# Layer 0's dependencies regrouped, and an expert's first 256 tokens multiplied with the down weights in seven block products instead of eight

## The chip, the cores and the metric

The kernel runs on one core of a Trainium2 chip. Its engines work at the same time, each through its own list of instructions in order: TensorE (PE) multiplies matrices, VectorE (DVE) and ScalarE (ACT) do elementwise work and read the results out of PSUM, GpSimd (POOL) issues gathers and scatters, and SyncE (SP) issues the plain transfers. They wait for each other by semaphores. The metric is the device time of one execution in microseconds (us), the median of several.

## The reference

The input is a matrix x of 625 nodes by 1024, and 10,625 edges (src, dst), among them a loop for every node. Two layers follow, each added to its input.

```
h    = layernorm(x)
h1   = relu(h @ W_self0 + mean(h) @ W_neigh0 + b0)
x    = x + h1 @ W_self1 + mean(h1) @ W_neigh1 + b1
f    = layernorm(x)
w    = softmax(f @ gate.T), kept for the two largest of 8 experts
out  = sum over experts e of w[:, e] * ((silu(f @ G[e].T) * (f @ U[e].T)) @ Dn[e].T)
x    = x + out + sigmoid(f @ s) * shared(f)
```

`mean` is the mean over a node's incoming edges. An expert has 1408 inner columns: G[e] and U[e] are 1408 x 1024, Dn[e] is 1024 x 1408. Everything is in f32.

## The kernel before

**Nodes and layer 0.** The 625 nodes lie in five tiles of 125. While PE multiplies the normalised rows with W_neigh0 (`rows_times`, tile y0), DVE writes one-hot rows of the edges, and PE counts edges between nodes with them, packed in digits. If a count does not fit its digit, the count is made anew in another way. So there is a region "count" with two cases, chosen by a register: case 1 recounts (`count_anew`, tile at), case 0 does nothing of it. In both cases PE multiplies the last rows of y0 (`last_rows`, eight products on bank 5), so that the choice has work beside it, and in case 0 ACT casts the counts c16 to bf16 (tile cb). Then h @ W_self0 is computed transposed (h1T) in seven block products for eight (`block_product`, bank p_h); DVE makes the sums of blocks for it (w3, b3 and in place), and y0 is split into three bf16 parts zh, zm, zl (`split`, with the scratch tiles yr). Region "sum0" then multiplies the parts with the counts: two halves of the nodes by eight groups of 128 columns, 15 matmuls a group; DVE scales each group by the reciprocal degree, adds it to h1T and takes the maximum with 0. Layer 1 follows in the same manner, from h1T, with the region "sum1".

**Experts.** One region for each of eight experts. Its case is the number of 64-token units that the expert has tokens for, from 0 (up to 64 tokens) to 7 (up to 512); `full` is the number of whole units of 128, and `odd` says that a half unit of 64 is left over. An expert's gathered rows are transposed into xg; the gate and up products fill ht (inner columns in 11 chunks of 128, tokens along the free dimension). The down stage multiplies ht with the weights wd, 11 chunks of 128 x 1024 that were loaded in full: first the half unit (`down_unit`), then the units from the last to the first (`down`, j = 3 to 0). A unit has two halves of 512 output columns, each 11 products into one bank; banks are 6 and 7, swapped if there is a half unit. ACT drains the first half, DVE the second, both with the routing weight as scale, into ys[j % 2] (the half unit uses ys[2]), and POOL scatters the unit's rows, adding to the output in memory. `CUT` parts the second half of unit 0: the weights' first six chunks are free once it has passed them, and SP then issues their loads for the next expert; the other five follow behind the region. The transposes of the next expert's first unit are put ahead of the down stage, on banks 2 and 3; those of its second unit come at the next region's start, on banks 4 and 5.

**Order and dependencies.** Python functions record all operations in one order (`Rec.op`); each engine gets its own in that order, and waits are derived from the tiles' bytes. In PSUM they go by bank: an operation waits for the last operation of every other engine on the bank, whether it reads or writes.

```
deps.update(o for e, o in m.bank[b].items() if e != eng or writing and eng != "PE")
```

A region's cases are recorded one beside the other and emitted as a branch. Since the case is not known before, an operation outside the case that depends on one inside waits for the end of its *segment* on that engine. `Rec.point` closes a segment: its end on an engine is the last instruction so far that the engine has in the region, and the counts of all cases are made equal there.

```
self.ends[self.segment, e] = self.add(eng=e, kind="end", members=[last[e] for last in self.last])
```

Ahead of each branch, `hint` names the case that will be taken. `mm` records each matmul by itself (the profile's line 539), `mm_all` (547) and `some_chunks` (1489) a whole group. In the profile 503, 504, 507 and 511 are DVE helpers, 515 and 520 ACT's, 1287 and 1356 gather and scatter.

Of the kernel before, what the change touches and what calls it, by code (L numbers as in the profile page):

```python
# [15 lines left out]
N = 625  # L16
# [15 lines left out]
NE = 8  # L32
FF = 1408
FC = FF // 128
SI = 176
SC = 2
SP = SI // SC
# [264 lines left out]
def gnn_moe(nc, x, src, dst, w_gnn0, w_gnn1, b0, b1, w_gu, w_down, ws_up, ws_down, out):  # L302
# [18 lines left out]
    def slot(i):  # L321
        return i * SLOT
# [66 lines left out]
    yr = [p(f"yr{i}", [TP, BANK]) for i in range(2)]  # L389
    p = space(slot(2), slot(8))  # L390
# [54 lines left out]
    power = power_i.bitcast(FP)  # L445

    wg = sb("wg", [128, FC, KD, 2, 128], FP, slot(0))
    wd = [sb(f"wd{c}", [128, D], FP, slot(2 * FC + c)) for c in range(FC)]
    p = space(R2, R4 + 20480)
    xg = p("xg", [128, KD, CAP])  # L450
    ht = p("ht", [128, FC, CAP])
# [3 lines left out]
    p = space(R1, R2)  # L455
    ys = [p(f"ys{i}", [128, D]) for i in range(3)]
    rows = [*(rows012[:, j, :] for j in range(3)), p("rows3", [128, XW])][:NTL]

    pa = pb("pa", 0, (128, NT, DIG))
    pg = pb("pg", 0, (128, NT, BANK))  # L460
# [39 lines left out]
    def ts(o, i, s1, s2, op0, op1=None):  # L500
        aps = [i] + [s for s in (s1, s2) if isinstance(s, bass.AP)]
        if op1 is None:
            return k.op("DVE", lambda h: h.tensor_scalar(o, i, s1, None, op0=op0), r=aps, w=[o])  # L503
        return k.op("DVE", lambda h: h.tensor_scalar(o, i, s1, s2, op0=op0, op1=op1), r=aps, w=[o])
# [4 lines left out]
    def stt(o, a, s, b, op0, op1):  # L509
        aps = [a, b] + ([s] if isinstance(s, bass.AP) else [])  # L510
        return k.op("DVE", lambda h: h.scalar_tensor_tensor(o, a, s, b, op0=op0, op1=op1), r=aps, w=[o])

    def copy(o, i, eng="DVE"):
        if eng == "ACT":
            return k.op("ACT", lambda h: h.copy(o, i), r=[i], w=[o])  # L515
        return k.op("DVE", lambda h: h.tensor_copy(o, i), r=[i], w=[o])  # L516
# [18 lines left out]
    def mm(o, pairs, start=True, stop=True):  # L535

        for n, (a, b) in enumerate(pairs):
            s, e = start and n == 0, stop and n == len(pairs) - 1
            k.op("PE", lambda h, a=a, b=b, s=s, e=e: h.matmul(o, a, b, start=s, stop=e, skip_group_check=True),  # L539
                 r=[a, b], w=[o])  # L540
# [302 lines left out]
    def node_half(m, n):  # L843
        return h1T[:, m, n * HB:min(N, n * HB + HB)]
# [39 lines left out]


    k.open("sum0", 2)
    turn = 0
    for k.cls in range(2):
        for n, (n0, nn) in enumerate(HALVES):
            for c in range(KD):  # L890
                q, o, t = bank("p_sum", 4 + turn % 4)[:, :nn], node_half(c, n), summed[turn % 2][:, :nn]
                turn += 1
# [12 lines left out]
    for c in range(KD):  # L905
        load(ws1[:, c, :], w_gnn1[c])
# [572 lines left out]

    FIRST, LAST = 2, 4  # L1480

    CUT = 6

    def some_chunks(o, pairs, lo, hi):

# [32 lines left out]
    def down(e, j, between, swap, stages):  # L1518
        y, w = ys[j % 2], gw[:, e % 2, j:j + 1]
        q = [bank("p_down", 7 - half if swap else 6 + half) for half in range(2)]  # L1520
        pairs = [[(ht[:, c, j * 128:(j + 1) * 128], wd[c][:, lo:lo + BANK]) for c in range(FC)] for lo in (0, BANK)]
        if 0 in stages:
            in_parts(q[:1], pairs[:1], between)
            act(y[:, :BANK], q[0], AF.Copy, scale=w)
            some_chunks(q[1:], pairs[1:], 0, CUT)
        if 1 in stages:
            some_chunks(q[1:], pairs[1:], CUT, FC)
            ts(y[:, BANK:], q[1], w, None, ALU.mult)

    SEG = -(-FC // 4)  # L1530
    for e in range(NE):
# [68 lines left out]
        if more:  # L1600
# [50 lines left out]
    def more(i):  # L1651
        return nc.If(nc.values_load(cnt_i[0:1, i:i + 1], min_val=0, max_val=N) > CAP)
# [65 lines left out]
```

## Time and profile before

| | us |
|---|---|
| median of 3 runs (lowest, highest) | 1123.2 (1121.39, 1125.63) |
| the profiled execution | 1122.52 |
| its span, first to last instruction | 1120.7 |
| PE busy in it | 1080.1 |
| DVE, ACT, POOL busy | 289.4, 127.5, 50.2 |
| layer 0, to the end of sum0's matmuls | about 202 |
| down stage of the expert with width 432 | 677.94 to 744.28 |
| down stages of the two experts with width 224 | 908.04 to 945.81, 1014.65 to 1052.42 |

The mean granted PE clock is 0.990. The timeline shows the eight experts' cases by their instructions: in order, 2, 0, 6, 1, 0, 3, 3 and 1. So three have two whole units or more: the third expert (width 432, three whole units and a half one) and the sixth and seventh (width 224, two whole units). In the profile a matmul on f32 is two records, with a weight load each. A line of the timeline gives the start, the duration, the engine, the line of the code, the operation and its tiles, and in brackets how long the engine had been idle and what ended that. "issue" means that the engine waited for nothing the profile can name.

### The profile page before, as it was taken

How to read it: one execution, taken by the hardware profiler on the slowest of the kernel's cores; microseconds unless marked ns; L12 is line 12 of the kernel's file. 1: busy time of each engine (PE TensorE's matmuls, PEld its weight loads, DVE VectorE, ACT ScalarE, POOL GpSimd, SP SyncE). 2: the span in 40 equal slices, each digit the busy share in tenths (PEclk: the TensorE clock that was granted, in tenths of full speed). 3: DMA queues.
4: the chain of work that ended last, by engine and by line, in shares of the span. 5: the costliest groups of instructions: out<-in, count | busy, mean ns of one | idle time of the engine just before them, and what ended most of it. 6: DMA issues, size and time to landing. Idle time of an engine off the chain costs nothing.

```text
span 1120.7 us, 10853 instructions
## 1 busy us (share of the span) xinstructions
PE 1080.1 (96%) x4265; PEld 617.0 (55%) x4265; DVE 289.4 (26%) x718; ACT 127.5 (11%) x246; POOL 50.2 (4%) x56
## 2 busy tenths in 40 slices
PE   6998999999999989999899999999989999999996
PEld 3554776444555544544455554445449965995452
DVE  7963555664644450001000000001010000000000
ACT  1122320122000231011100000001010000000010
POOL 0000000000000040001000000100100001000001
PEclk9999999999999989999899999999999999999998
DMA  9600012302033239869953033168799644642601
GB/s 302 244 1 5 0 40 73 151 0 80 1 133 128 74 124 331 323 266 347 405 202 150 7 144 123 19 212 354 264 407 364 252 177 150 230 187 114 214 34 26
DMA packets 40874, 186.53 MB, mean 166 GB/s; under 512 B 6933, under 2 KB 6933, under 8 KB 29300
## 3 DMA queue, kind: packets, MB, share of 16 engines
q1 hardware_dynamic: 34432, 168.18, 38.9%
q0 software_dynamic: 6000, 16.26, 6.3%
q8 instruction: 62, 1.02, 0.4%
q14 instruction: 120, 0.98, 0.3%
q10 hardware_dynamic: 260, 0.09, 0.0%
HBM read 170.51 MB, written 13.99 MB: 165 GB/s over the span
## 4 chain that ended last, share of the span: by engine, by line
PE 92%; DVE 3%; issue 3%; ACT 1%; DMA 1%; POOL 0%; SPq 0%; POOLq 0%; ACTq 0%; DVEq 0%
PE p_gu L547 34%; PE p_down L1489 20%; PE p_y L539 11%; PE p_h L539 5%; PE p_sage L539 5%; PE p_gu L1422 5%; PE p_sum L539 5%; PE p_gs L539 2%; PE p_downs L539 1%; PE pa L656 1%; PE p_gu L597 1%; PE p_tr L597 1%; DVE ln_st L554 1%; DMA rows<-xfw,idx 0%; DMA xa<-in_x_dram 0%
## 5 line engine op out<-in xcount | busy, mean ns | idle before, releaser
L547 PE MATMUL p_gu<-xg,wg 128*128 128x224 f32 (+1 forms) x1056 | 264.2, 413 | 0.4 <-ACT xg L515 0.2
L547 PEld LDWEIGHTS p_gu<-xg,wg 128*128 128x128 f32 x1056 | 201.3, 191 | 62.8 <-issue 61.4
L1489 PE MATMUL p_down<-wd,ht 128*128 128x512 f32 (+1 forms) x616 | 229.5, 594 | 0.0
L1489 PEld LDWEIGHTS p_down<-wd,ht 128*128 128x128 f32 (+1 forms) x616 | 95.0, 175 | 125.0 <-issue 124.8
L507 DVE TENSOR_TENSOR ht<-ht,p_gu 128x256 f32<-128x256 f32 (+3 forms) x63 | 27.4, 437 | 368.9 <-PE p_gu L547 231.8
L547 PE MATMUL p_gu<-wg,xg 128*128 128x512 f32 (+1 forms) x288 | 116.8, 565 | 0.9 <-DVE ht L507 0.6
L547 PEld LDWEIGHTS p_gu<-wg,xg 128*128 128x128 f32 x288 | 55.1, 193 | 60.1 <-issue 57.7
L539 PE MATMUL p_y<-wn,h0T 128*125 128x512 f32 x160 | 72.8, 610 | 1.3 <-ACT h0T L515 1.3
L520 ACT ACTIVATE ht<-p_gu 128x256 f32<-128x256 f32 (+3 forms) x63 | 25.0, 396 | 428.7 <-PE p_gu L547 357.8
L1422 PE MATMUL p_gu<-wg,xg 128*64 128x512 f32 (+2 forms) x384 | 58.3, 461 | 0.5 <-ACT xg L515 0.5
L503 DVE TENSOR_SCALAR ys<-p_down,gw 128x512 f32<-128x512 f32 x10 | 7.5, 751 | 182.6 <-PE p_down L1489 182.6
L539 PE MATMUL p_h<-h0T,ws 128*128 128x313 f32 x192 | 51.1, 426 | 3.4 <-issue 3.4
L539 PEld LDWEIGHTS p_y<-wn,h0T 128*125 128x125 f32 x160 | 30.1, 193 | 37.9 <-issue 35.2
L539 PEld LDWEIGHTS p_h<-h0T,ws 128*128 128x128 f32 x192 | 36.2, 189 | 18.4 <-issue 4.2
L1356 POOL DMA_INDIRECT out_dram<-ys,idx x13 | 19.9, 1532 | 556.6 <-DVE ys L503 320.8
L1422 PEld LDWEIGHTS p_gu<-wg,xg 128*64 128x64 f32 x384 | 25.5, 137 | 32.1 <-issue 28.1
L539 PE MATMUL p_y<-wn,h1T 128*125 128x512 f32 x96 | 41.6, 593 | 1.5 <-DVE h1T L503 1.5
L539 PE MATMUL p_sage<-ws,h1T 128*125 128x512 f32 x96 | 41.9, 592 | 0.0
L503 DVE TENSOR_SCALAR os<-node,src_f 125x640 f16<-125x640 f16 x85 | 32.2, 379 | 3.0 <-PE pa L656 3.0
L539 PEld LDWEIGHTS p_y<-wn,h1T 128*125 128x125 f32 x96 | 17.9, 188 | 24.5 <-issue 22.2
L539 PEld LDWEIGHTS p_sage<-ws,h1T 128*125 128x125 f32 x96 | 17.9, 187 | 22.1 <-issue 21.8
L539 PE MATMUL p_gs<-wus,xfT 128*125 128x361 f32 x80 | 25.2, 467 | 0.4 <-DVE xfT L516 0.4
(202 smaller groups left out, 778.2 us busy)
## 6 DMA issues: line engine op xcount, KB each, us to landing
wg<-in_w_gu_dram SPq DMA_DIRECT2D x88, 1024.0 KB, 10.8
wd<-in_w_down_dram SPq DMA_DIRECT2D x88, 512.0 KB, 9.5
wn<-in_w_gnn_dram SPq DMA_DIRECT2D x16, 512.0 KB, 13.8
ws<-in_w_gnn_dram SPq DMA_DIRECT2D x16, 512.0 KB, 13.5
xr<-in_x_dram SPq DMA_DIRECT2D x5, 448.0 KB
xfw<-xf SPq DMA_DIRECT2D x5, 448.0 KB
out_dram<-xr SPq DMA_DIRECT2D x5, 448.0 KB
xa<-in_x_dram SPq DMA_DIRECT2D x4, 448.0 KB
```

Of the source, the lines that this page charges most:

```text
L503: return k.op("DVE", lambda h: h.tensor_scalar(o, i, s1, None, op0=op0), r=aps, w=[o])
L507: return k.op("DVE", lambda h: h.tensor_tensor(o, a, b, op), r=[a, b], w=[o])
L520: return k.op("ACT", lambda h: h.activation(o, i, f, **kw), r=aps, w=[o])
L539: k.op("PE", lambda h, a=a, b=b, s=s, e=e: h.matmul(o, a, b, start=s, stop=e, skip_group_check=True), r=[a, b], w=[o])
L547: got = h.matmul(o if m is None else o[:, :m], a, b if m is None else b[:, :m], start=start and n == 0, stop=stop and n == len(pairs) - 1, ...
L554: k.op("DVE", lambda h, part=part, st=st: h.bn_stats(st, part), r=[part], w=[st])
L597: got = h.transpose(pt[:, c, :], i[:n, (4 * g + c) * 128:(4 * g + c + 1) * 128], ident[:n, :n])
L656: k.op("PE", lambda h, s=s: h.matmul(pa[:, s, :], o_s[:, s, :], o_d[:, :DIG], start=c == 0 and s == 0, stop=c == EC - 1 and s == NT - 1, s ...
L1356: h.indirect_dma_start(out=to, out_offset=bass.IndirectOffsetOnAxis(ap=i, axis=0), in_=y, in_offset=None, compute_op=ALU.add).then_inc(s, 16)
L1422: got = h.matmul(o, *pairs[n], start=n == 0, stop=n == len(pairs) - 1, skip_group_check=True)
L1489: got = h.matmul(o[job], *pairs[job][n], start=n == 0, stop=n == FC - 1, skip_group_check=True)
```

## The change

**Layer 0.** Four edits. `last_rows` is cut in two by inner chunks: the first four chunks stay in the count region's first segment, the other four come in a second segment that both cases share, with a one-element copy on DVE so that the engine has an end there. The cast to cb comes before the last rows' copy, and cb lies at R3 now, over the recount's tile at, instead of over the weights wn0. yr moves to slot 7, and deg_row, w3, b3 and the tiles `summed` from slot 2 to slot 0. Region sum0 is ordered by halves outside and cases inside, with a segment end behind each half, and its groups go round all eight banks instead of four.

**Down stage.** If an expert has two whole units or more, units 1 and 0 are multiplied together (`down_pair`). The 256 tokens by 10 chunks of ht and the 10 chunks by 1024 columns of wd are each cut in 2 x 2 blocks (128 tokens, 5 chunks, 512 columns), and seven products of sums of blocks replace eight products of blocks. DVE makes the sums, most of them in place in ht and wd, e3 in a new tile and the fifth block difference d3 in parts of xg that are free by then. The eleventh chunk is multiplied in the plain way, one product for each of the four blocks of the result. The first product's bank z (6) is drained three times into ys as a beginning, is added to by the second product and drained once more; the others (x, y, w: banks 4, 5, 7) are added to ys by DVE with the routing weight. Stage 0 uses the weights' first five chunks for the last time, so `CUT` becomes 5 for all. Units 3 and 2 and the half unit are as before. Unit 1's scatter is issued behind unit 0's end, next to unit 0's.

```
-    p = space(slot(0), slot(8))
-    cb = p("cb", [TP, NT, N], BF)
+    cb = sb("cb", [TP, NT, N], BF, R3)
+    p = space(slot(0), slot(8))
...
-    def last_rows():
+    def last_rows(part):
         q = bank("p_y", 5)[:TP, :]
-        mm(q, [(h0T[:, c, N - TP:N], wn0[:, c, BANK:]) for c in range(KD)])
-        copy(y0[:, NT - 1, BANK:], q, "ACT")
+        mm(q, [(h0T[:, c, N - TP:N], wn0[:, c, BANK:]) for c in range(KQ * part, KQ * part + KQ)], part == 0, part == 1)
+        if part:
+            copy(y0[:, NT - 1, BANK:], q, "ACT")
...
     count_anew()
-    last_rows()
+    last_rows(0)
     k.cls = 0
     copy(ok[:, 1:2], ok[:, 0:1])
-    last_rows()
     copy(cb, c16[:, :, :N], "ACT")
+    last_rows(0)
+    k.cls = None
+    k.point()
+    for k.cls in range(2):
+        last_rows(1)
+        copy(ok[:, 2:3], ok[:, 0:1])
...
-    for k.cls in range(2):
-        for n, (n0, nn) in enumerate(HALVES):
+    for n, (n0, nn) in enumerate(HALVES):
+        for k.cls in range(2):
             for c in range(KD):
-                q, o, t = bank("p_sum", 4 + turn % 4)[:, :nn], node_half(c, n), summed[turn % 2][:, :nn]
+                q, o, t = bank("p_sum", (4 + c) % 8)[:, :nn], node_half(c, n), summed[c % 2][:, :nn]
...
-    k.cls = None
-    k.point()
+        k.cls = None
+        k.point()
...
-    CUT = 6
+    CUT = FD
...
+    def down_pair(e, stages):
+        a11, a12, a21, a22 = (ht[:, i:i + FD, t:t + 128] for t in (0, 128) for i in (0, FD))
+        b11, b12, b21, b22 = (wd_all[:, i:i + FD, n:n + BANK] for i in (0, FD) for n in (0, BANK))
+        x, y, w, z = (bank("p_down", b) for b in (4, 5, 7, 6))
...
+        if 0 in stages:
+            tt(e3, a11, a21, ALU.subtract)
+            tt(a21, a21, a22, ALU.add)
+            for i, o in enumerate(d3):
...
+                    tt(o, hi, lo, ALU.subtract)
+            product(z, a11, b11, True)
+            act(place(0, 1), z, AF.Copy, scale=by[0])
+            ts(place(1, 0), z, by[1], None, ALU.mult)
+            act(place(1, 1), z, AF.Copy, scale=by[1])
+            tt(b12, b12, b11, ALU.subtract)
+            product(z, a12, b21, False, (0, 0))
+            act(place(0, 0), z, AF.Copy, scale=by[0])
+            tt(a11, a21, a11, ALU.subtract)
+            tt(b11, b22, b12, ALU.subtract)
+            tt(a12, a12, a11, ALU.subtract)
+            tt(b21, b21, b11, ALU.subtract)
+            product(y, a21, b12, True)
+            more(1, 1, y)
+            product(x, a11, b11, True)
+            more(0, 1, x)
+            product(w, None, None, True, (1, 1))
+            more(1, 1, w)
+        if 1 in stages:
+            product(x, e3, d3, False)
+            more(1, 1, x)
+            product(y, a12, b22, False, (0, 1))
+            more(0, 1, y)
+            product(x, a22, b21, False, (1, 0))
+            more(1, 0, x)
...
-        for j, stages in ((None, (0, 1)), *((j, (0, 1)) for j in range(NTL - 1, 0, -1)), (0, (0,)), (0, (1,))):
+        for j, stages in ((None, (0, 1)), *((j, (0, 1)) for j in range(NTL - 1, 1, -1)), (0, (0,)), (0, (1,))):
...
+                elif j == 0 and full > 1:
+                    down_pair(e, stages)
...
-                now.append(scatter(e, j, half))
+                now += [scatter(e, i, half) for i in ((0, 1) if j == 0 else (j,))]
```

Here `tt` is a sum or difference on DVE, `ts` and `act` scale a bank into a tile on DVE and ACT, `place(j, half)` is a half of ys[j], `more(j, half, q)` adds bank q, scaled, to it on DVE, and `product(q, a, b, start, last)` multiplies two blocks into a bank, with the eleventh chunk's product behind them if `last` is given.

More of the change, by code (lines that the diff above doesn't have):

```diff
@@ L34 @@
 FC = FF // 128
+FD = FC // 2
 SI = 176
@@ L385, in gnn_moe @@
     t3 = p("t3", [128, KQ, BANK])
+    cb = sb("cb", [TP, NT, N], BF, R3)
     p = space(slot(0), slot(8))
-    cb = p("cb", [TP, NT, N], BF)
     yh, ym = (p(n, [TP, NT, D], BF) for n in ("yh", "ym"))
-    yr = [p(f"yr{i}", [TP, BANK]) for i in range(2)]
-    p = space(slot(2), slot(8))
+    yr = [sb(f"yr{i}", [TP, BANK], FP, slot(7) + 2048 * i) for i in range(2)]
+    p = space(slot(0), slot(8))
     deg_row, w3, b3 = p("deg_row", [128, N]), p("w3", [128, KQ, BANK]), p("b3", [128, KQ, HB])
@@ L447, in gnn_moe @@
     wg = sb("wg", [128, FC, KD, 2, 128], FP, slot(0))
-    wd = [sb(f"wd{c}", [128, D], FP, slot(2 * FC + c)) for c in range(FC)]
+    wd_all = sb("wd", [128, FC, D], FP, slot(2 * FC))
+    wd = [wd_all[:, c, :] for c in range(FC)]
     p = space(R2, R4 + 20480)
@@ L457, in gnn_moe @@
     rows = [*(rows012[:, j, :] for j in range(3)), p("rows3", [128, XW])][:NTL]
+    e3 = p("e3", [128, FD, 128])
+    d3 = [xg[:, 2 * i:2 * i + 2, 128:384] for i in range(4)] + [xg[:, :4, 384:]]
     pa = pb("pa", 0, (128, NT, DIG))
@@ L886, in gnn_moe @@
     k.open("sum0", 2)
-    turn = 0
-    for k.cls in range(2):
-        for n, (n0, nn) in enumerate(HALVES):
+    for n, (n0, nn) in enumerate(HALVES):
+        for k.cls in range(2):
             for c in range(KD):
-                q, o, t = bank("p_sum", 4 + turn % 4)[:, :nn], node_half(c, n), summed[turn % 2][:, :nn]
-                turn += 1
+                q, o, t = bank("p_sum", (4 + c) % 8)[:, :nn], node_half(c, n), summed[c % 2][:, :nn]
                 cols = slice(c * 128, (c + 1) * 128)
@@ L1528, in down, with product, place, more @@
             ts(y[:, BANK:], q[1], w, None, ALU.mult)
+    def down_pair(e, stages):
+        a11, a12, a21, a22 = (ht[:, i:i + FD, t:t + 128] for t in (0, 128) for i in (0, FD))
+        b11, b12, b21, b22 = (wd_all[:, i:i + FD, n:n + BANK] for i in (0, FD) for n in (0, BANK))
+        x, y, w, z = (bank("p_down", b) for b in (4, 5, 7, 6))
+        by = [gw[:, e % 2, j:j + 1] for j in range(2)]
+        def product(q, a, b, start, last=None):
+            pairs = [(a[:, i, :], b[i] if isinstance(b, list) else b[:, i, :]) for i in range(FD)] if a is not None else []
+            if last is not None:
+                j, half = last
+                pairs.append((ht[:, FC - 1, 128 * j:128 * j + 128], wd[FC - 1][:, half * BANK:half * BANK + BANK]))
+            mm_all(q, pairs, start=start)
+        def place(j, half):
+            return ys[j][:, half * BANK:half * BANK + BANK]
+        def more(j, half, q):
+            o = place(j, half)
+            stt(o, q, by[j], o, ALU.mult, ALU.add)
+        if 0 in stages:
+            tt(e3, a11, a21, ALU.subtract)
+            tt(a21, a21, a22, ALU.add)
+            for i, o in enumerate(d3):
+                if i in (0, 4):
+                    m = 4 if i == 0 else 1
+                    o = xg[:, :, 128:384] if i == 0 else o
+                    o = o.rearrange("p (k a) b -> p k a b", k=m)
+                    hi, lo = (b[:, i:i + m, :].rearrange("p k (a b) -> p k a b", b=o.shape[-1]) for b in (b22, b12))
+                    tt(o, hi, lo, ALU.subtract)
[23 more added lines that the diff above has]
+            more(1, 0, x)
```

## The prediction, made before the result was known

> **What bounds the kernel now.** I read the page's busy times and its chain first: they say which engine sets the end, and whether anything else can be on the path.
>
> ```profile
> PE 1080.1 (96%) x4265; PEld 617.0 (55%) x4265; DVE 289.4 (26%) x718; ACT 127.5 (11%) x246; POOL 50.2 (4%) x56
> ...
> PE 92%; DVE 3%; issue 3%; ACT 1%; DMA 1%; POOL 0%; SPq 0%; POOLq 0%; ACTq 0%; DVEq 0%
> ```
>
> The matmul engine carries 92% of the chain. So the change can win in two ways: fewer matmuls, or less time in which PE stands still. The list of what PE waited for prices the second way.
>
> ```profile
> PE p_xg L597 <- issue: 7.5, 2, 4.0
> PE p_h L539 <- issue: 3.4, 1, 3.4
> ...
> PE p_y L539 <- DVE h1T L503: 1.5, 1, 1.5
> PE p_sum L539 <- DVE summed L507: 1.4, 1, 1.4
> ```
>
> Three of these lie in layer 0, which the change touches: 3.4, 1.5 and 1.4 us. The first says "issue", which names no releaser, so I looked at the other engines in time order around it.
>
> ```profile
> 105.74 0.58 ACT L515 COPY y<-p_y 125x512 f32<-125x512 f32 x1 [6.28 <-PE p_y L539]
> ...
> 106.22 2.80 ACT L515 CAST cb<-c 125x3125 bf16<-125x3125 f16 x1
> ...
> 109.12 17.09 PE L539 MATMUL p_h<-h0T,ws 128*128 128x313 f32 x64 [3.42 <-issue]
> ```
>
> The cast to cb ends at 109.02 and PE goes on at 109.12. In the code p_h takes banks that the recount (the other case of the region) drains on ACT, and after a region such a dependency is on the segment's last ACT instruction: the cast. PE waits for cb, which it needs only 60 us later.
>
> Last, the down stages of the experts with two full units or more. The timeline shows three: the expert at 547 us (width 432, three full units and a half one), and those at 840 and 947 us (width 224, two).
>
> ```profile
> 706.72 0.75 DVE L503 TENSOR_SCALAR ys<-p_down,gw 128x512 f32<-128x512 f32 x1 [17.56 <-PE p_down L1489]
> ...
> 708.31 1.57 POOL L1356 DMA_INDIRECT out_dram<-ys,idx  x1 [14.16 <-DVE ys L503]
> ...
> 744.28 16.04 PE L547 MATMUL p_gu<-wg,xg 128*128 128x512 f32 x37
> ...
> 908.04 37.93 PE L1489 MATMUL p_down<-wd,ht 128*128 128x512 f32 x88
> ...
> 945.81 1.04 PE L597 MATMUL p_xg<-ident,rows 128*128 128x128 f32 x8
> ...
> 946.01 0.75 DVE L503 TENSOR_SCALAR ys<-p_down,gw 128x512 f32<-128x512 f32 x1 [18.13 <-PE p_down L1489]
> ```
>
> The 44 products of two units appear as 88 records (each f32 product is two) from 908.04 to 945.81 without idle: 0.429 us a record, 0.858 us a product. A drain sees PE's end 0.20 to 0.25 us late (945.81 to 946.01).
>
> **The change, part by part. Count region.** The cast to cb moves ahead of the last rows' copy and into a segment of its own, to a place that waits for no weights. ACT ends the copy before it at 99.45 (98.87 + 0.58), so the cast can run from 99.5 to 102.3, or to 106 at worst if the entry into the case costs the 4 us that DVE's entry into the same region had at most (hint and entry lay beside a 4.07 us reciprocal, with no idle behind). PE ends the last rows at about 105.6. So p_h starts between 105.6 and 106.1: a gain of 3.0 to 3.5, taken as 3.4. DVE's sums (w3 and the rest, 7.5 us in four) start 3 us earlier; PE had 13 us of products before it needs them, so that is worth nothing. The extra one-element copy on DVE is 0.11 us in an idle stretch; the split rows are the same 16 records.
>
> **Sum region.** PE stops after four groups because DVE takes the first only at 177.25, 7 us after it is ready; four banks are then full. Eight banks hold 16 us of groups (2.0 us each), and DVE, at 1.28 us a group, catches up at about the tenth. The 1.4 us go. The 1.5 us behind the region stay: splitting by halves frees h1T's first half, but the next product writes banks 6 and 7, which the second half's groups used too, so it still waits for the segment's last DVE instruction. Bounds 1.4 to 2.9; I take 1.4. Layer 0 together: **-4.8 us**.
>
> **Pair, PE.** Seven blocks of 5 chunks and four products of the eleventh chunk are 39 products for 44: 5 x 0.858 = -4.3 us each time, -12.9 in three experts. **DVE** gains four sums of 640 columns (0.80, from the 128x625 row), 2048 + 512 columns for the differences (2.29 + 0.69), three of 2560 (2.29 plus 512 columns at the 1.04 ns between the 2048 and 1252 rows: 2.82), one scaled copy and six accumulations of 0.75: about 20 us, beside 33 us of PE work. None but the first lies on the path: y needs a21 and b12, ready 3 us before; x needs b11, ready 4 us before. If DVE ran at half this rate, z's drain would come 4 us later and x wait 2 more.
>
> **Seam after the first product.** Bank z must be drained three times (ACT, DVE, ACT) before the second product adds to it, and the recorder orders any two engines that touch one bank, reads too. Layer 1 shows this:
>
> ```profile
> 221.79 0.58 ACT L515 COPY y<-p_y 125x512 f32<-125x512 f32 x1
> ...
> 222.53 0.68 DVE L516 COPY y<-p_y 125x512 f32<-125x512 f32 x1
> ...
> 223.25 0.58 ACT L515 COPY y<-p_y 125x512 f32<-125x512 f32 x1 [0.88 <-DVE y L516]
> ```
>
> The third waits for the second. Here the drains scale: 0.69 + 0.75 + 0.69, with 0.25 ahead and 0.13 of handing on: PE idles 2.5 us. DVE's sums ahead of its drain end at about 912.85 in the expert at 840 us, 0.45 before its turn. Behind it, x's second use waits 0.1 (a drain of 0.95 beside one product of 0.86). So a pair is worth -4.3 + 2.6 = **-1.7 us** where nothing else is late: the expert at 947 us.
>
> **Expert at 840 us.** Its successor begins with transposes into bank 4, which is now x: they wait for the last accumulation, 0.95 us. **-0.7 us.**
>
> **Expert at 547 us.** Two things stand ahead. z is bank 6, where unit 2's second half lies, so PE waits for its drain (706.72 + 0.75): 1.05 us. Then ACT's first drain writes ys[0], which unit 2's scatter is still reading: issued at 708.31, its last packets run to about 714.2 in the transfer view. Before, unit 1's 19 us lay between. Behind ACT stand the DVE drain, all of DVE's sums, and PE. ACT goes at 714.2 instead of 712.1, the second product starts at 716.45 instead of 711.8: 4.65 us idle. Sum: -4.3 + 1.05 + 4.65 + 0.1 = **+1.5**. The scatters' range from issue to landing, 4.5 to 11.1 us, makes this 0.1 to 6.7; the row itself gives 5.9.
>
> **Clock.** An idle of 4.65 us can drop the granted clock. After the stops at 539.5 (3.95 us) and 834.3 (3.50) it fell to half; after the 3.42 us at 105.7 it did not:
>
> ```profile
> 109.00:110.00 1.00, 0.88 (x4) 0.68 (x5) 1.00 (x1) 0.02 (x1) 0.00 (x0) 1.00 0.00 0
> ...
> 838.00:839.00 1.00, 1.00 (x7) 1.00 (x6) 0.00 (x0) 0.00 (x0) 0.21 (x1) 0.50 0.98 393
> ...
> 841.00:842.00 1.00, 1.00 (x6) 0.97 (x5) 0.00 (x0) 0.00 (x0) 0.77 (x1) 0.84 1.01 332
> ```
>
> The third column from the end is the clock: half from 838 to about 841.4, which costs 1.7 us; the other stop ran at half from 544.6 to 551.1, 3.2 us. Bounds 0 to 3.2; I take **+1.7**, since 4.65 is longer than both stops that dropped it. [...]
>
> **Queues.** Unit 1's scatter moves behind unit 0's: POOL issues two in a row (1.55 us each) and the next gather comes at most 1.6 later; it waits for DVE's gw copies anyway (953.38, 4.24 idle before it) and is needed 60 us on: nothing. SP loads five down chunks (0.65 us each) instead of six after the first stage, and six after the region; in pairs that is 15 us before the end instead of 4: nothing in long experts. Before the two experts with one half unit the first loads start 0.86 earlier beside PE's change of code: 0 to 0.5 each, taken as 0 because the same overlap cost nothing at 508.4. In the last expert a skipped scatter stands before the last real one; two skipped gathers cost 0.72 - 0.30 at 409.9, so **+0.2**.
>
> **Sum.** -4.8 - 1.7 - 0.7 + 1.5 + 1.7 + 0.2 = -3.8. The profiled execution took 1122.5 (span 1120.7 and 1.8 around it): 1118.7. It stands 0.7 under the median of the runs shown, 1123.2.
>
> **The rivals.** *The seams are cheaper:* no drop of the clock, and the scatter lands at its best, 4.5 us (1.4 less): 1115.6. For it: the 3.42 us row. Against: two of three such stops dropped. *The count gap stays:* if leaving the region is itself a code fetch of 3 us, layer 0 gives only 1.4: 1122.1. For it: "issue" as releaser; against: the cast's end, 0.10 before. [...]
>
> **How the numbers follow.** 0.5% is 5.6 us, about what a measurement can tell from no change. Forecast 0.50, own range 1116.0 to 1121.5; cheaper seams 0.26; count gap stays 0.10; code fetch 0.14. Faster by over 0.5%: nearly all of the second (0.24) and a quarter of the first (0.12), together 0.36. Slower: the last, 0.14. The rest, 0.50, is within. The range 1114.0 to 1124.0 leaves out the code fetch and a twentieth below.
>
> **What would show it.** p_h starting within 0.5 us of the last rows; no PE wait for "summed"; a PE wait of about 1.5 for h1T as before; 78 records a pair, with one stop of about 2.5 us in two experts and of 1.0 plus 4.6 in the one at 547 us, ACT's first drain there behind "DMA out_dram"; half clock after that stop. Wrong would be: PE stops at y or x (DVE's rate), or stops over 1 us behind the pairs (code fetch).

## The result, and the profile after

The changed kernel takes 1143.5 us (median of four executions, 1141.11 to 1143.79); the kernel before took 1123.7 beside it (1121.39 to 1125.63). The ratio is 1.0165 with a 95% interval of 1.0146 to 1.0183: slower by 1.65%, where 1118.7 us was forecast. The profiled execution took 1143.66 us, its span is 1141.8 us, and the mean granted clock of TensorE (PE) is 0.978 where it was 0.990.

The page's busy times and its chain, engine by engine:

```profile
PE 1074.4 (94%) x4235; PEld 613.0 (54%) x4235; DVE 343.1 (30%) x761; ACT 129.7 (11%) x249; POOL 50.8 (4%) x56
...
PE 89%; DVE 3%; another core or an unknown queue 2%; issue 2%; DMA 1%; ACT 1%; POOL 0%; SPq 0%; POOLq 0%; ACTq 0%; DVEq 0%
```

PE is busy for 5.7 us less, and the span is 21.1 us longer. The chain has an entry that was not there: 2%, "another core or an unknown queue", two stretches of 12.96 and 12.86 us. The list of waits of the changed kernel (engine, line, tile, what it waited for: total, times, longest) names the instructions that stand beside it:

```profile
ACT ys L525 <- DMA out_dram<-ys,idx: 66.2, 5, 17.4
...
PE p_down L552 <- ACT ys L525: 28.8, 3, 11.7
```

PE stops three times after a pair's first product, 28.8 us in all, and ACT, which drains that product, waits for a scatter into the output. The stages of the two profiled executions side by side, each from the start of its first PE record to that of the next stage:

| stage | before, us | after, us | difference | predicted |
|---|---|---|---|---|
| layer 0, to the product behind sum0 | 203.40 | 198.54 | -4.9 | -4.8 |
| third expert, down | 66.34 | 71.86 | +5.5 | +1.5, and +1.7 for the clock |
| sixth expert, down | 37.77 | 48.41 | +10.6 | -0.7 |
| seventh expert, down | 37.77 | 48.43 | +10.7 | -1.7 |
| behind it, to the end | 68.28 | 68.65 | +0.4 | +0.2 |
| stages between, not touched | | | -1.2 | 0 |

The sum is +21.1 us. The stages between are -2.7 us up to the third expert's down stage and +1.4 behind it; the first of these stretches takes 471.9 us here and 474.7 us in a run below that has the same PE work, so this is no effect of the change. Two stages hold the whole loss, and in both the stop was predicted at 2.5 us (the sixth expert is the prediction's "expert at 840 us", the seventh the one at 947 us, the third the one at 547 us). Here is the sixth expert in order of time (start, duration, engine and line; in brackets the idle time before and what ended it):

```profile
907.41 4.46 PE L552 MATMUL p_down<-wd,ht 128*128 128x512 f32 x10
921.30 0.69 ACT L525 ACTIVATE ys<-p_down,gw 128x512 f32<-128x512 f32 x1 [13.05 <-DMA out_dram<-ys,idx]
922.02 0.75 DVE L508 TENSOR_SCALAR ys<-p_down,gw 128x512 f32<-128x512 f32 x1 [9.81 <-ACT ys L525]
922.80 0.69 ACT L525 ACTIVATE ys<-p_down,gw 128x512 f32<-128x512 f32 x1 [0.82 <-DVE ys L508]
923.54 16.59 PE L552 MATMUL p_down<-wd,ht 128*128 128x512 f32 x34 [11.68 <-ACT ys L525]
```

The first product is done at 911.87. The three drains take 0.69 + 0.75 + 0.69 us one behind the other, as predicted. But the first of them starts at 921.30, 9.4 us late. It writes ys[0], and what it waits for is a scatter of ys[0] that moves nothing: this expert has two whole units, so the scatter of unit 2 is skipped, and GpSimd (POOL) gives the credit for it (the semaphore count that says that the rows have been read) in its place, by hand. Its instruction queue, by the lines of the code that lead to that credit (durations are ns, minimum/median/maximum, then first and last start):

```profile
L1370 POOLq MOVE  x2: 29/29/29, 908.0 to 908.0; - x2
L1370 POOLq COMPARE_BRANCH  x2: 43/54/65, 908.1 to 914.0; - x2
L1370 POOLq BRANCH_PREFETCH_HINT  x1: 41/41/41, 913.5 to 913.5; - x1
L1372 POOLq INC_SWDGE_SEM  x1: 406/406/406, 913.6 to 913.6; - x1
L1376 POOLq COMPARE_BRANCH  x2: 50/53/56, 919.9 to 920.6; - x2
L1382 POOLq INC_SWDGE_SEM  x2: 428/438/447, 920.1 to 920.8; - x2
```

POOL comes to the odd unit's scatter first, whose case is chosen by a jump table (L1370, a Switch over the eight unit counts). Between its compare at 908.1 and the next instruction at 913.5 lie 5.3 us, and between its last compare at 914.0 and the branch of the next scatter at 919.9 another 5.9. The credits of units 3 and 2 follow at 920.1 and 920.8 (L1382), and ACT goes at 921.30. In the seventh expert the same two stretches lie at 1025.5 to 1030.7 and 1031.3 to 1037.0, and ACT goes at 1038.51.

The kernel before had a wait of this kind too. In its timeline:

```profile
921.08 0.69 ACT L520 ACTIVATE ys<-p_down,gw 128x512 f32<-128x512 f32 x1 [12.20 <-DMA out_dram<-ys,idx]
```

That is the stage's first drain, of unit 1 into ys[1], and it waits for the credit of the skipped scatter of unit 3, which stands behind the same table (in that trace POOL's stretches are 908.8 to 914.3 and 914.9 to 920.4). PE had filled its bank by 917.5, eleven products after 908.04, and went on with the other half's bank; it needs the first bank again only after another 9.4 us. So the drain was 3.5 us late and PE never met the wait. In the pair the stage's first drain comes after five products, it writes ys[0], whose credit is one place further back, and PE's very next instruction, the second product, adds to the bank that is being drained.

The stop has a second price. The granted clock of PE ahead of it and behind it in the sixth expert (window, PE busy, clock in the third column from the end):

```profile
908.00:911.00 3.00, 3.00 (x9) 1.00 0.71 229
924.00:926.00 2.00, 2.00 (x3) 0.50 0.00 0
926.00:928.00 2.00, 2.00 (x5) 0.73 0.00 0
928.00:930.00 2.00, 2.00 (x6) 1.00 0.00 0
```

The seventh expert shows 0.50 from 1041 to 1046, the third 0.50 from 710 to 715. The 34 records behind the stop took 16.59, 17.71 and 17.50 us in the sixth, the seventh and the third expert, where they take 14.86 at a clock of 1.00 (below): 1.7, 2.9 and 2.6 us. Thus the sixth expert: 4.0 us less for the records (37.77 against 33.74 for a pair without stops, below), 11.7 of stop, 1.7 of clock and 0.8 for the next expert's bank 4: 10.2 of the 10.6.

### The profile page after: what moved, and what is told of

Same layout as the page of the kernel before. It is cut to its first block, busy times and chain, and to the rows that moved or that the text cites. A ratio compares the mean times of both kernels' runs of the same rounds, so it can differ in the third digit from the quotient of the medians.

```text
span 1141.8 us, 10839 instructions
## 1 busy us (share of the span) xinstructions
PE 1074.4 (94%) x4235; PEld 613.0 (54%) x4235; DVE 343.1 (30%) x761; ACT 129.7 (11%) x249; POOL 50.8 (4%) x56
## 4 chain that ended last, share of the span: by engine, by line
PE 89%; DVE 3%; another core or an unknown queue 2%; issue 2%; DMA 1%; ACT 1%; POOL 0%; SPq 0%; POOLq 0%; ACTq 0%; DVEq 0%
PE p_gu L552 33%; PE p_y L544 11%; PE p_down L1498 9%; PE p_down L552 8%; PE p_sum L544 6%; PE p_h L544 5%; PE p_sage L544 5%; PE p_gu L1431 5%; PE p_gs L544 2%; PE p_downs L544 1%; PE pa L661 1%; PE p_gu L602 1%; DMA out_dram<-ys,idx 1%; PE p_tr L602 1%
## 5 line engine op out<-in xcount | busy, mean ns | idle before, releaser
L552 PE MATMUL p_down<-wd,ht 128*128 128x512 f32 x204 | 96.7, 633 | 29.6 <-ACT ys L525 28.8
L1498 PE MATMUL p_down<-wd,ht 128*64 128x512 f32 (+1 forms) x352 | 115.9, 595 | 0.0
L552 PEld LDWEIGHTS p_down<-wd,ht 128*128 128x128 f32 x204 | 41.0, 204 | 83.4 <-issue 49.7
L1498 PEld LDWEIGHTS p_down<-wd,ht 128*64 128x64 f32 (+1 forms) x352 | 45.0, 163 | 62.8 <-issue 62.6
L544 PEld LDWEIGHTS p_y<-wn,h1T 128*125 128x125 f32 x96 | 17.9, 187 | 24.5 <-issue 22.2
```

Source lines behind the costliest of these rows:

```text
L552: got = h.matmul(o if m is None else o[:, :m], a, b if m is None else b[:, :m], start=start and n == 0, stop=stop and n == len(pairs) - 1, ...
L1498: got = h.matmul(o[job], *pairs[job][n], start=n == 0, stop=n == FC - 1, skip_group_check=True)
```

## The experiments

The theory after the result: the whole loss comes from ACT's first drain, which waits for the credit of a skipped scatter, and this credit is late because POOL passes the jump table before it. Rivals: the two parts of the change disturb each other; ACT itself is late; POOL's order is no matter. Ratios are against the kernel before, run on the same chip; its median was 1124.2 in the first four runs, 1124.6 in the next four and 1122.8 in the last three.

### Each part alone

Layer 0's edits alone, with the down stage and CUT of before:

```
-    CUT = FD
+    CUT = 6
...
-        for j, stages in ((None, (0, 1)), *((j, (0, 1)) for j in range(NTL - 1, 1, -1)), (0, (0,)), (0, (1,))):
+        for j, stages in ((None, (0, 1)), *((j, (0, 1)) for j in range(NTL - 1, 0, -1)), (0, (0,)), (0, (1,))):
...
-                elif j == 0 and full > 1:
-                    down_pair(e, stages)
...
-                now += [scatter(e, i, half) for i in ((0, 1) if j == 0 else (j,))]
+                now.append(scatter(e, j, half))
```

> Layer 0's edits alone, down stage as before. Changed kernel's trace: h1T's last use by the next product starts at 198.54 us instead of 203.40, 4.9 earlier. If nothing gives this back, 1123.7 - 4.9 = 1118.8. If something behind layer 0 takes it back (a transfer that is late anyway), 1121 to 1123.7.

Measured: 1117.6 us, ratio 0.9947 (0.9929 to 0.9966). The second kernel has the pair alone, on the layer 0 of before (the diff of layer 0 undone).

> The paired down stage alone, layer 0 as before. If the two parts are independent: 1143.5 + 4.9 = 1148.4. If the loss came from layer 0's edits (cb's new place, the moved tiles), it would be near 1124.

Measured: 1148.4 us (two executions), ratio 1.0221 (1.0188 to 1.0254). By the ratios layer 0 is worth about -6 us and the pair about +25; -5.3 per mille and +22.1 add up to +16.8 where the whole change measured +16.5. So the parts do not disturb each other beyond what these intervals leave (some 2 to 3 per mille), layer 0 did what it was to do, and the loss is the pair's. PE's waits in the pair alone, with layer 0's stop of 3.4 us back in its place:

```profile
PE p_down L552 <- ACT ys L525: 27.9, 3, 11.5
...
PE p_h L544 <- issue: 3.4, 1, 3.4
```

### First drains into memory that no scatter reads

The pair's first drains and running sums go to columns of ht that an expert's pair doesn't use (`held`), and only the last accumulation of each place writes ys. The same products, drains and banks; only the wait's cause is gone.

```
+        def held(j, half):
+            i = 2 * (2 * j + half)
+            return ht[:, i:i + 2, 256:512]
...
-        def more(j, half, q):
-            o = place(j, half)
-            stt(o, q, by[j], o, ALU.mult, ALU.add)
+        def more(j, half, q, last=False):
+            i = held(j, half)
+            stt(two(place(j, half)) if last else i, two(q), by[j], i, ALU.mult, ALU.add)
...
-            act(place(0, 1), z, AF.Copy, scale=by[0])
+            act(held(0, 1), two(z), AF.Copy, scale=by[0])
```

> Changed kernel, but the first drains and the running sums go to columns of ht that are free by then; ys is written only by the last accumulation of each quarter. Theory of POOL's credit (PE waits for ACT, ACT for the release of ys[0] by this expert's skipped scatter): the stops of 11.7, 11.6 and 5.5 us behind the first product become 2.5 each, and the half clock behind them goes (34 records in 16.6, 17.7 and 17.5 us become 14.7): 1143.5 - 21.3 - 7.7 = 1114.5. Rival, ACT's own delay (code or a table for the scaled copy): the stops stay, 1143.5. Rival, the drains serialised on one bank are the loss: unchanged too, since the bank and its three drains stay.

Measured: 1117.0 us, ratio 0.9942 (0.9923 to 0.9962), 26 us under the changed kernel. The sixth expert, in order of time:

```profile
905.20 0.69 ACT L525 ACTIVATE ht<-p_down,gw 128x512 f32<-128x512 f32 x1 [3.65 <-PE p_down L552]
905.92 0.75 DVE L508 TENSOR_SCALAR ht<-p_down,gw 128x512 f32<-128x512 f32 x1 [0.42 <-ACT ht L525]
906.70 0.69 ACT L525 ACTIVATE ht<-p_down,gw 128x512 f32<-128x512 f32 x1 [0.82 <-DVE ht L508]
907.44 14.86 PE L552 MATMUL p_down<-wd,ht 128*128 128x512 f32 x34 [2.28 <-ACT ht L525]
914.08 0.69 ACT L525 ACTIVATE ys<-p_down,gw 128x512 f32<-128x512 f32 x1 [6.69 <-DMA out_dram<-ys,idx]
```

The first drain now starts when PE is done, and PE stops for 2.28 us, in all three experts, with the clock at 1.00 behind it (706 to 710, 908 to 912 and 1014 to 1016). ACT's drain at 914.08, which goes into ys as before, still waits for the scatter's credit, 6.69 us, and nobody on PE's path waits for it. The wait on ys is thus the cause, and ACT is not late by itself. The 2.5 us above the expectation are within what the executions of this kernel spread: the profiled one took 1114.0 us at a mean clock of 0.990, the longest 1121.8 at 0.984.

### Eighty empty instructions on POOL

In the sixth and the seventh expert POOL gets 80 empty instructions between the skipped scatter of the half unit and that of unit 3.

```
             for half in halves_of:
                 now += [scatter(e, i, half) for i in ((0, 1) if j == 0 else (j,))]
+            if j is None and e in (5, 6):
+                for _ in range(80):
+                    k.op("POOL", lambda h: h.nop())
```

> Changed kernel with 80 empty instructions on POOL in the sixth and seventh expert, between the half unit's skipped scatter and unit 3's. Theory of POOL's credit: each of the two stops grows by what these take on POOL, some 3.4 us if one costs 43 ns as a compare does, so about 1150. Rival, the credit waits for the memory queue behind the weight loads, or ACT is late by itself: 1143.5, as POOL has time.

Measured: 1143.0 us, ratio 1.0173 (1.0151 to 1.0195): no change. The stops are 11.2, 11.6 and 5.2 us in the sixth, the seventh and the third expert. A miss, and no evidence against the theory: the trace has no record of the empty instructions on POOL's queue, and the distance from the odd unit's credit to the next branch (914.9 to 920.8) is 5.9 us, where it is 6.3 without them (913.6 to 919.9). They delayed nothing, so this run tells nothing of what a delay would do.

### The jump table replaced

The same cases, reached by nested two-way branches.

```
-                for n in h.Switch(tokens(e), UNITS):
-                    if n % 2 or n == 0:
-                        h.inc_swdge_sem([s], [16])
-                    else:
-                        go(h, s, ys[2][:64, some], i[:64, n // 2:n // 2 + 1])
+                def pick(n):
+                    if n == 0:
+                        h.inc_swdge_sem([s], [16])
+                        return
+                    with h.If(tokens(e) > n - 1):
+                        if n % 2:
+                            h.inc_swdge_sem([s], [16])
+                        else:
+                            go(h, s, ys[2][:64, some], i[:64, n // 2:n // 2 + 1])
+                    with h.Else():
+                        pick(n - 1)
+                pick(UNITS - 1)
```

> The whole change, with the jump table of the odd unit's scatter replaced by nested two-way branches that lead to the same instructions. Base: the changed kernel at about 1143.3 us where the kernel before has 1124. Theory (ACT's first drain waits for the credit of the skipped scatter of unit 2, and that credit stands on GpSimd behind two stretches of 5.3 and 5.9 us that belong to the jump table): with near branches the credit comes some 11 us sooner, TensorE's stops in the experts at 840 and 947 us fall from 11.6 to about 2.3 us and the half clock behind them goes: 1143.3 - 2 x (9.3 + 2.2) = about 1120 us. Rival 1 (any jump out of a recorded branch costs such a stretch, whatever its form; with four units three levels are passed): 16 us or more ahead of the credit, stops of 16 us, about 1155 us. Rival 2 (the stretches have nothing to do with the branch's form: the return to straight code costs them): stops and time as they are, 1143 us.

Measured: 1120.2 us, ratio 0.9971 (0.9957 to 0.9985). POOL's queue in the sixth expert:

```profile
L1374 POOLq COMPARE_BRANCH  x6: 38/45/45, 908.0 to 909.1; - x6
L1376 POOLq INC_SWDGE_SEM  x1: 397/397/397, 908.7 to 908.7; - x1
L1383 POOLq COMPARE_BRANCH  x2: 45/45/45, 909.3 to 910.0; - x2
L1389 POOLq INC_SWDGE_SEM  x2: 433/434/434, 909.5 to 910.2; - x2
```

From 908.0 to 910.6, where the jump table needed 908.0 to 921.3. ACT's first drain starts at 911.89, straight behind PE, and PE goes on at 914.13:

```profile
911.89 0.69 ACT L525 ACTIVATE ys<-p_down,gw 128x512 f32<-128x512 f32 x1 [3.65 <-PE p_down L552]
...
914.13 11.43 PE L552 MATMUL p_down<-wd,ht 128*128 128x512 f32 x26 [2.29 <-ACT ys L525]
```

So the two stretches belong to the jump table; rivals 1 and 2 fall. With this one edit, on POOL alone, the down stages of the sixth and the seventh expert take 37.29 and 36.28 us, 0.5 and 1.5 less than before where 0.7 and 1.7 were predicted, and the whole change stands at 1120.2 us where 1118.7 was forecast.

### The jump table behind the credit

The jump table stays, but the odd unit's scatter is issued behind that of unit 2.

```
-                now += [scatter(e, i, half) for i in ((0, 1) if j == 0 else (j,))]
+                now += [scatter(e, i, half) for i in {None: (), 2: (2, None), 0: (0, 1)}.get(j, (j,))]
```

> The whole change, with the odd unit's scatter (the one with the jump table) put behind the scatter of unit 2 on GpSimd instead of ahead of the scatters of units 3 and 2. Theory (unit 2's credit is late because GpSimd passes the jump table first): the credit is given before the jump table. If nothing else precedes it, TensorE's stops in the experts at 840 and 947 us fall from 11.6 to 2.3 us and the time to about 1143.3 - 23 = 1120 us; if one stretch of 5.5 us of code still precedes it (ACT then starts near 915 us where TensorE ended the first half at 912), to 4 to 5 us and about 1128 us. The third expert, where unit 2's scatter is a real one, can gain up to 3.2 us more (5.5 to 2.3). Rival (ACT's drain waits for something else than GpSimd's order, or for the earlier expert's scatters): the stops stay at 11.6 us and the time at 1143 us.

Measured: 1121.7 us, ratio 0.9983 (0.9968 to 0.9999). POOL's queue in the sixth expert, credits first and the table behind them:

```profile
L1376 POOLq COMPARE_BRANCH  x2: 45/45/45, 907.9 to 908.5; - x2
L1382 POOLq INC_SWDGE_SEM  x2: 392/410/429, 908.0 to 908.7; - x2
L1370 POOLq COMPARE_BRANCH  x2: 43/54/65, 909.3 to 915.1; - x2
L1370 POOLq BRANCH_PREFETCH_HINT  x1: 41/41/41, 914.6 to 914.6; - x1
```

The table is as slow as ever (its compare at 909.3, the next instruction at 914.6), and costs nothing there. PE's stops in the two experts are 2.28 and 2.29 us. This, more than the run before it, shows that it is the order that counts. The further 3.2 us hoped for in the third expert did not come: PE stops there for 5.56 us, as before, since POOL's real scatter of unit 2 was never behind the table; it is issued at 700.36, when its rows are ready, and ACT, which waits for it, starts at 707.43, 7 us behind.

### The same edit in the kernel before

The nested branches in the kernel before, with nothing else.

> The kernel before, with nested two-way branches for the jump table and nothing else changed. Theory (ACT's late drain at 921 us was there before the change and hidden behind other products): ACT's waits of 12 us for the credit go, and the time stays at 1124 us, ratio 1.000 within 0.002. Rival (the wait was already part of the time before): 3 to 10 us less.

Measured: 1124.2 us, ratio 1.0012 (1.0000 to 1.0025). In the kernel before ACT's list of waits has

```profile
ACT ys L520 <- DMA out_dram<-ys,idx: 47.5, 4, 12.3
```

These four waits are gone from the trace of the variant, and the time stays. The wait was there before and cost nothing.

### The seams that are left

Three more kernels go on from the one with the free columns. The first changes only the order of the pair's banks:

```
-        x, y, w, z = (bank("p_down", b) for b in (4, 5, 7, 6))
+        x, y, w, z = (bank("p_down", b) for b in (7, 6, 5, 4))
```

> The variant with the first drains in unused columns (1117.0 us where the kernel before had 1124.2), with the four PSUM banks of the pair in the order 7, 6, 5, 4 instead of 4, 5, 7, 6. Theory: the first product no longer opens the bank that the unit before it has just filled (the wait of 0.84 us on bank 6 in the third expert goes) and the last no longer leaves the bank that the next region opens first (0.84 us, the wait of the next expert's gathered tokens on bank 4, goes): 1.7 us less, 1115.3 us. Rival (TensorE's short waits at the borders are covered by other short waits behind them): 1117 us, within 0.5.

Measured: 1114.9 us, ratio 0.9920 (0.9891 to 0.9948). Both waits of 0.84 us are gone from the trace; the intervals of the two kernels overlap, so the time alone doesn't show the 2 us. In the profiled execution the clock dropped behind two of the three stops, though they are no longer than before (0.50 from 705 to 707, 0.65 over 910 to 914, and 1.00 over 1016 to 1020):

```profile
704.76 16.46 PE L552 MATMUL p_down<-wd,ht 128*128 128x512 f32 x34 [2.28 <-ACT ht L525]
...
908.99 16.55 PE L552 MATMUL p_down<-wd,ht 128*128 128x512 f32 x34 [2.29 <-ACT ht L525]
...
1015.81 14.86 PE L552 MATMUL p_down<-wd,ht 128*128 128x512 f32 x34 [2.29 <-ACT ht L525]
```

The second gives the second product a bank of its own, so that PE waits for no drain in the middle of the pair:

```
-            product(z, a12, b21, False, (0, 0))
-            act(place(0, 0), z, AF.Copy, scale=by[0])
+            act(held(0, 0), two(z), AF.Copy, scale=by[0])
+            product(w, a12, b21, True, (0, 0))
...
             more(1, 1, y)
+            more(0, 0, w, True)
```

> As the run with the other bank order, and the second product is accumulated in its own bank instead of on top of the first one, whose sum is drained to all four places: the TensorE stop of 2.28 us after the first product, three times, goes, for one more drain on VectorE (0.75 us) that no TensorE instruction waits for. Theory: 3 x 2.28 = 6.8 us less than that run, about 1108.5 us where the kernel before has 1124. Rival 1 (a later bank's drain becomes the wait, since w is opened once more after (0, 0) has been drained from it behind VectorE's differences): stops of 1 to 2 us come back at the last product, about 1112 us. Rival 2 (VectorE's differences, which are later behind the extra drain, hold the third product): about 1113 us.

Measured: 1108.1 us, ratio 0.9846 (0.9822 to 0.9869). No wait of a pair is left on PE:

```profile
900.85 19.05 PE L552 MATMUL p_down<-wd,ht 128*128 128x512 f32 x44
919.89 4.56 PE L552 MATMUL p_down<-xg,e 128*128 128x512 f32 x10
924.28 10.46 PE L552 MATMUL p_down<-wd,ht 128*128 128x512 f32 x24
934.59 1.04 PE L602 MATMUL p_xg<-ident,rows 128*128 128x128 f32 x8
```

A pair now takes 33.74 us, 4.0 less than the 37.77 of before; neither a later drain nor DVE's sums hold anything. The third changes banks in layer 0's sum, so that the product behind it needs only the first half's drains:

```
-                q, o, t = bank("p_sum", (4 + c) % 8)[:, :nn], node_half(c, n), summed[c % 2][:, :nn]
+                q, o, t = bank("p_sum", ((4, 5, 6, 7, 0, 1, 2, 3), (4, 5, 0, 1, 2, 3, 4, 5))[n][c])[:, :nn], node_half(c, n), summed[c % 2][:, :nn]
```

> As the variant with the second product in its own bank (1108.1 us), and the second half of layer 0's sum uses the banks 4, 5, 0 to 5 instead of 4 to 7, 0 to 3, so that the product behind it, on banks 6 and 7, needs only the first half's drains. Theory of the prediction (the 1.4 us stop of that product stays because its banks are the ones that the second half uses): the stop goes and the time falls by 1.4 us, to 1106.7 us. Rival (the product waits for the rows that it multiplies, which the second half has to finish, and the bank is no matter): stop and time as they are, 1108.1 us.

Measured: 1104.8 us, ratio 0.9848 (0.9825 to 0.9871). "PE p_y <- DVE h1T: 1.4" is gone from its list of waits, and the first drain of that product starts at 203.20 where it started at 204.84, with p_h starting at 105.10 and 105.02. So the stop was the banks', as the prediction said, and 1.7 us are gained there. The ratio is that of the run before, so the whole time doesn't resolve it.

The last one has all of these and the nested branches.

> As the run with the other banks in layer 0's sum, and nested two-way branches for the jump table. Theory (the jump table costs only what waits for a credit behind it; with the first drains in unused columns nothing on TensorE's path does): the same time as that run, within 2 us. Rival (the long stretches on GpSimd also disturb what runs beside them or lengthen the tail): more than 2 us less.

Measured: 1105.0 us, ratio 0.9843 (0.9825 to 0.9860): the same. With nothing on PE's path waiting for a credit, the jump table costs nothing that these intervals (2 to 3 us either way) show. The last three variants take 1.5% less than the kernel before.

## Why the prediction was wrong

**The step that failed** is the pair's worth: "So a pair is worth -4.3 + 2.6 = -1.7 us where nothing else is late: the expert at 947 us." Something else was late. The prediction checked ACT's drain into ys[0] against the scatter that reads ys[0] only in the third expert, where that scatter moves data. In the other two it has no term for the skipped one, as if a skipped scatter were no scatter. But ACT waits for its credit all the same, POOL gives credits in the order of its queue, and ahead of this one stand the jump table's 11 us. The row that says so was in the trace of before (the drain at 921.08 that waits 12.20 us, one of four such waits, 47.5 us in all); it was hidden there by the products on the other bank, and the pair puts PE's next instruction directly behind that first drain. The wait is 9.4 and 9.3 us in the two experts, and 1.7 and 2.9 of half clock behind them: 23.3 in all. The run with the nested branches removes just that: its two down stages are 11.1 and 12.2 us shorter than the changed kernel's in the traces, and it takes 23.3 us less by the medians, some 22 by the ratios to the kernel before.

**Layer 0.** Right. p_h starts at 105.90 without a wait (predicted 105.6 to 106.1); the wait for "summed" is gone; the 1.4 us for h1T stay, and for the reason given, the banks. -4.9 us in the trace against -4.8; about -6 by the ratio of the run with this part alone, whose interval is -3.8 to -8.0.

**PE's products.** 78 records, as predicted, and 4.0 us saved in a pair without stops where 4.3 was said. **DVE** has 53.7 us more, 17.9 a pair (predicted about 20), and nothing waits for its sums.

**The seam.** 2.28 us where 2.5 was said (in the variants where the first drain waits for nothing), three drains in series; the shape of the run of drains is that of the rows from layer 1. **Bank 4** cost 0.84 (predicted 0.95) and **bank 6** 0.84 (1.05).

**Third expert.** The mechanism was right, ACT's drain behind the real scatter, and its size too small: 5.52 us instead of 4.65. The scatter's issue took 2.07 us (1.57 before), with DVE busy beside it, and ACT goes 7.06 us after the issue, not 5.9:

```profile
700.77 2.07 POOL L1365 DMA_INDIRECT out_dram<-ys,idx  x1 [14.12 <-DVE e L512]
...
707.83 0.69 ACT L525 ACTIVATE ys<-p_down,gw 128x512 f32<-128x512 f32 x1 [17.40 <-DMA out_dram<-ys,idx]
...
710.07 17.50 PE L552 MATMUL p_down<-wd,ht 128*128 128x512 f32 x34 [5.52 <-ACT ys L525]
```

Whether DVE is what lengthens the issue no run shows. With the half clock (2.6 us, predicted 1.7) the stage is at +5.5, not +3.2.

**Clock.** One drop of half clock was predicted and three came, behind 5.5, 11.6 and 11.7 us. The stops of 2.28 us with a drop (two, in the run with the other order of banks) and that of 3.42 without one (in the kernel before) show that here the length alone doesn't decide it.

**Rivals.** The count gap went, the seams were not cheaper in the third expert, and no stop over 1 us came behind the pairs (0.85 us is the longest), so what the prediction gave 0.14 as "code fetch", time lost on PE there, did not happen. That PE fetches code between experts no run shows: its stops there stand in the traces as "issue" (3.95 and 3.50 us in the kernel before, 4.07 and 3.58 in the changed one). Time was lost at a branch, but on POOL, which the prediction put at nothing: under "Queues" it counted POOL's real issues in the pairs and not the branches around the skipped ones. The chance for slower, 0.14, stood for another mechanism than the one that came, and the range, up to 1124.0, left even that one out.

**What stays open.** That the jump table's form costs the 11 us is shown; why is not. There are 5.3 us going into the table's case and 5.9 coming out of it, and no such stretch at the nested branches, six compares of 38 to 45 ns between 908.0 and 909.1. The profile has a DMA queue that it calls "instruction", which moves fewer packets with nested branches than with the table (packets, MB, share of 16 engines):

```profile
q14 instruction: 120, 0.98, 0.3%
...
q14 instruction: 88, 0.72, 0.2%
```

The first line is the changed kernel's, the second that of the run with nested branches. In the sixth expert of the changed kernel one such packet falls in the first stretch and two in the second. And the table was faster where the DMA engines were nearly idle. In the last expert of the kernel before, the four stretches of two tables take 2.5 to 2.8 us each, at a DMA share of 0.02 to 0.04; in its sixth and seventh expert they take 5.3 to 5.7 us, at 0.46 to 0.92. That POOL waits for such packets in the stretches would fit these figures and is the author's inference: no view names what a packet brings or who waits for it, and no run changed the load alone. What a longer delay on POOL would cost wasn't measured either, as the empty instructions delayed nothing.

## What to carry to other kernels

A skipped transfer is not a transfer that never was: here ACT, which overwrites its source, waited for its credit and started 9.4 and 9.3 us late, since the credit came in the order of POOL's queue, behind a branch that took 5.3 and 5.9 us. Before an instruction is moved to the front of a stage, read in the trace what it waits for where it stands, even if nobody waits for it there: a wait of 12 us that is hidden is a price for whoever takes its cover away. The cure need not be where the loss is seen: another place for the first sums, another order of two scatters, or another form of a branch each took the stops of 11.6 us away.

## What the runs showed of the hardware

- A jump table on POOL took 5.2 to 5.5 us to enter and 5.5 to 5.9 us to leave in the sixth and the seventh expert, beside the weight loads (DMA share 0.46 to 0.92 in the kernel before), and 2.5 to 2.8 us each in the last expert, with hardly a transfer beside it (0.02 to 0.04); in the sixth expert the same choice by nested branches took about 1.3 us in all (908.0 to 909.3), with 0.4 us of it the credit.
- A credit given by hand took 0.39 to 0.45 us of POOL's queue in the sixth expert.
- A stop of PE of 2.28 us behind a pair's first product was followed by half clock in two of three places in one execution, at 1.6 to 1.7 us each, and in none of seven in three others (34 records in 14.86 us); behind stops of 5.2 us and more in that place the 34 records took 16.59 to 17.78 us in all eight cases that four executions show, 1.7 to 2.9 more, and the clock of the three in the changed kernel was 0.50 at first.
- POOL's issue of a scatter of 128 rows took 2.07 us while DVE was busy with the block sums, and 1.57 without them.
